# Four 64x64 products at a step's head for the last taps of two layers

## The chip, the cores and the metric

The kernel runs on one core of a Trainium2 chip. The core has five engines that run side by side, each through its own list of instructions in order: TensorE (PE in the profile, its weight loads PEld), VectorE (DVE), ScalarE (ACT), GpSimd (POOL) and SyncE (SP), which here issues most of the transfers. They wait for each other through semaphores. The metric is the device time of one execution in microseconds; the time of a version is the median of its runs.

## What is computed

Input x has 16 images of 64 channels of 128x128, in float32. Four layers follow, each a residual step on a group norm (`_gn`, 32 groups):

```python
x = x + _L0_conv_ref(_gn(x), conv_w)      # gram matrix of the channels, its product with x, a 64x64 mix
x = x + _L1_conv_ref(_gn(x))              # |Sobel x| + |Sobel y| of each channel
x = x + _L2_conv_ref(_gn(x), W, b)        # shift of channel groups by one column, 3x3 convolution
x = x + _L3_conv_ref(_gn(x), w_bin, ...)  # 3x3 convolution, 1x1, batch norm over all images, clip
```

Layer 3's batch norm needs all images, so the output can only be made in a closing pass over everything.

## The kernel before

An image is cut into eight pieces of rows (`NS` = 8), one per step. A long pipeline runs over the steps (loop at line 1059); in each step three stages work at different images or pieces: `Front` (layers 0 and 1) from step 15, `Layer2` from step 25, `Layer3` from step 35, each eight steps per image; the last of layer 3 is step 162. `Gram` prepares layer 0 for later images. A step has four quarters `q` = 0 to 3; in each quarter the stages run in the order Layer3, Layer2, Front, then Gram, and each engine keeps the order in which the program issues. After every quarter `tick` (264) advances the short chains that make the norms' coefficients.

- **Front.** From image 3 on (`self.four`, line 555) `mix_four` (579) mixes one piece in quarter 1: four products on 64x64 tiles of TensorE, written to the PSUM tiles `po` and `g`, which have one buffer each. `prepare` (598) lets ScalarE normalize them into `xh`: half 0 in quarter 2, half 1 in quarter 0 of the next step. The image's edge lines `pe` are handled once per image. `sobel` (657) is VectorE's work of layer 1 in all quarters, with the two absolute values on ScalarE.
- **Layers 2 and 3.** The 3x3 convolution over row pairs is rewritten with a product shared by both rows (`shared`, 750, into `one`) and two of its own (`own`, 753, into the two halves of `two`), on differences of rows (`diffs`, tiles `d2` and `d3`, made by `difference` on VectorE). Each product exists for two column halves of TensorE, and two halves of different sides run as a pair at a time; `issue` (730) pairs them and holds a rest back until a partner comes. In each `own`, one side has three taps. The other side reads only one row plane, that is half of the contraction; two of its taps are packed into one product (`pk`) with the help of a shifted copy (`twins`, tiles `qd`), and the last tap remains as a product of its own with half of its weights zero. `pk` and this last tap are the two entries of `some[o]` (line 757 on).
- **Twins.** Layer 3's are copied by ScalarE (952): two copies in quarter 3, two in quarter 0. Layer 2's come by two transfers on GpSimd's queue (810), after VectorE has made the difference: half 0 in quarter 0, half 1 at the end of quarter 3.
- **Order on TensorE in a step:** layer 3's shared and first own products (quarter 0), its second (1), the mixing (1), Gram products if any, layer 2's shared and one own (2), its other own (3).
- **Order on ScalarE:** quarter 0: two `qd<-d` copies, `xh` half 1, `junk<-u`; quarter 1: `c` of layer 3, `v` of layers 3 and 2; quarter 2: two absolute values, `c` of layer 2, `junk<-x`, `xh` half 0; quarter 3: two `qd<-d` copies, `junk<-y`. Copies `xw` for the Gram products come in between.
- **Order on VectorE:** quarter 0: two Sobel operations, the edge addition `two<-two,edges` and layer 2's result `x<-two,c`, `d2`; quarter 1: four Sobel operations; quarter 2: layer 3's result `y<-two,c`, `d3`, Sobel; quarter 3: `d3`, Sobel, `d2`.

The tiles `two` have two buffers, taken in turn by layers 3 and 2. Nearly all instructions go through the helper class `InOrder`, so the profile puts them at its line 73.

Of the kernel before, what the change touches and what calls it, by code (L numbers as in the profile page):

```python
# [16 lines left out]
P = 128  # L17
# [3 lines left out]
R = 8  # L21
# [23 lines left out]
def single(table, n):  # L45

    for o in range(2):
        planes = [i for m, i, half, _ in table if (m, half) == (n, o)]
        if len(planes) == 1:
# [3 lines left out]

NAMES = [("I", P), ("same", P), ("all", P), ("gavg", P), ("gmean", P), ("bnavg", P), ("Id", C), ("q", 1),
         ("keep0", 1), ("keep1", 1), ("left", 1), ("right", 1), ("I3", 3 * P), ("lower", 1), ("upper", 1)]
# [22 lines left out]
def constants():  # L78
    k = np.zeros((P, K_END), np.float32)
    p = np.arange(P)  # L80
    ch = p % C

    def put(name, a):
        k[:, AT[name][0]:AT[name][1]] = a

    same = ch[:, None] == ch[None, :]
    pair = ch[:, None] // 2 == ch[None, :] // 2
    put("I", np.eye(P))
    put("same", same)
    put("all", np.full((P, P), 0.5))  # L90
    put("gavg", 0.25 * pair)
    put("gmean", pair / (2.0 * HW))
    put("bnavg", (ch[:, None] == (p // 2)[None, :]) / (B * HW))
    put("Id", ch[:, None] == np.arange(C)[None, :])
    put("q", 0.25)
    put("keep0", (~((ch >= C // 4) & (ch < C // 2)))[:, None])
    put("keep1", (~(ch < C // 4))[:, None])

    left, right = ch < C // 4, (ch >= C // 4) & (ch < C // 2)
    put("left", left[:, None])  # L100
    put("right", right[:, None])
    put("I3", np.concatenate([np.eye(P) * m[:, None] for m in (left, ~left & ~right, right)], axis=1))
    put("lower", (p < C)[:, None])
    put("upper", (p >= C)[:, None])
    return k
# [3 lines left out]
def tile_kernel(ctx: ExitStack, tc: tile.TileContext, x, cw_h, w2_t, b2, wbin_t, w1_t, b1, gamma, beta, consts, out):  # L109
# [10 lines left out]
    def k(name):  # L120
        return kc[:, AT[name][0]:AT[name][1]]

# [96 lines left out]
    for name in ("d2", "d3"):  # L219
        diffs[name] = wpool.tile([P, 2, CP, W + 2], F32, name=name)  # L220
        pool.memset(diffs[name], 0.0)
        twins[name] = wpool.tile([P, 2, CP, W + 2], F32, name=f"q{name}")
        pool.memset(twins[name], 0.0)
# [10 lines left out]

    wm = wpool.tile([P, 3, P], F32, name="wm")
    packed = {}

    def other_weights():
        for n in range(2):
            o = 1 - single(TO_SLOTS, n)[0]  # L240
            pool.tensor_copy(wm[:, :, cols(o)], w2[:, n, :, cols(o)])

        for name, w, table in (("pk2", w2, TO_SLOTS), ("pk3", w3, TO_PAIRS)):
            dve.tensor_add(w[:, 2], w[:, 0], w[:, 1])
            packed[name] = wpool.tile([P, 2, C], F32, name=name)
            for n in range(2):
                o, i = single(table, n)
                for kx, half in ((1, i), (0, 1 - i)):
                    pool.tensor_copy(
                        packed[name][half * C:(half + 1) * C, n], w[i * C:(i + 1) * C, n, kx, o * C:(o + 1) * C]  # L250
                    )
# [17 lines left out]

    def rstd(mE, r, me, eps=None):  # L270

        dve.tensor_copy(me, mE)
        nv = sv("nv")
# [14 lines left out]
    def coefficients(st, put, back=None):  # L288
# [5 lines left out]
        pm = sm(2)  # L294
        small_product(pm, k("gmean"), s2)
        yield
        co = sv("co", 2) if back is None else sv("co2", 6)
        me = sv("me", 2)
        r, mean = co[:, 0:1], me[:, 0:1]
        yield from rstd(pm, r, me, GN_EPS)  # L300
        dve.scalar_tensor_tensor(co[:, 1:2], mean, -1.0, r, op0=ALU.mult, op1=ALU.mult)
# [11 lines left out]
    def gram_chain(b, pg):  # L313
# [21 lines left out]

        junk0 = stp.tile([P, C], F32, tag="junk0", name=f"junk0_{b}", bufs=1)
        dve.scalar_tensor_tensor(
# [56 lines left out]
        yield  # L394
        pp = stp.tile([P, 2, C], F32, tag="pp", name=f"pp_{b}", bufs=1)
        dve.tensor_mul(
# [152 lines left out]
    class Front:  # L549
# [29 lines left out]
        def mix_four(self, i):  # L579
# [3 lines left out]
            t = self.xs.pop(i)  # L583
            order = 1 - last[0], last[0]
            for g in range(2):
                for h in order:
                    pe.matmul(self.po[i, g][cols(h)], self.abd[cols(g), cols(g)], t[cols(g), h], start=True, stop=True)

# [17 lines left out]
        def at(self, i, q):  # L606
            b = self.b
            if q == 0:
# [6 lines left out]
                if i + 3 < NS and i + 3 not in self.xs:  # L615
                    self.load(i + 3)
                if -1 <= i < NS - 1:
                    self.prepare(i + 1, 1)
# [6 lines left out]
                if i == NS:  # L625
                    chains.append(coefficients(self.st, lambda co: coefs2.update({b: co}), b2_sb))
            if q == 1 and -2 <= i < NS - 2:
                if i == -2:
                    self.abd, self.co = lead.pop(b)
                if i == -2 and not self.four:  # L630
                    self.pe = ps_g.tile([P, CP, W], F32, tag="g", name=f"pe_{b}")[:, 0, :]
                    small_product(self.pe, self.abd, self.xe)
                if self.four:
                    self.mix_four(i + 2)
                else:
                    self.mix(i + 2, 0)
            if q == 3 and i == -2 and self.four:
                self.pe = ps_po.tile([P, CP, W], F32, tag="po", name=f"pe_{b}")[:, 0, :]
                small_product(self.pe, self.abd, self.xe)
            if (i, q) == ((-1, 0) if self.four else (-2, 2)):  # L640
                nc.gpsimd.memset(self.chunk(0)[lo, 0, :], 0.0)
# [3 lines left out]
            if q == 2:  # L645
                if i == NS - 2:
                    nc.gpsimd.memset(self.chunk(NS - 1)[hi, R + 1, :], 0.0)
                    act.copy(self.chunk(NS - 1)[lo, R + 1, 1:1 + W], self.pel[lo])
            if 0 <= i < NS:
                self.sobel(i, q)  # L650
            if q == 2 and -2 <= i < NS - 2:
                self.prepare(i + 2, 0)
            if q == 3 and -2 <= i < NS - 2 and not self.four:
                self.mix(i + 2, 1)
                self.xs.pop(i + 2)

# [72 lines left out]

    def issue(halves):  # L730


        for o in range(2):
            for n, (dst, wt, src) in enumerate(halves[o]):
                held[o].append((dst, wt, src, n == 0, n + 1 == len(halves[o])))
        while held[0] and held[1]:
            o = 1 - last[0]
            emit(o)
            emit(1 - o)
# [12 lines left out]

    def own(p, n, table, wt, name, m=CP, both=None):
        d, q, pk = diffs[name][:, n, 0:m], twins[name][:, n, 0:m], packed[f"pk{name[1]}"][:, n]
        o, _ = single(table, n)
        some = [None, None]
        some[1 - o] = taps(1 - o, p[:, 0:m], [wt[:, n] if both is None else both], [d], 1)
        some[o] = [
            (p[cols(o), 0:m], pk, q[:, :, 1:1 + W]),
            (p[cols(o), 0:m, 0:W - 1], wt[:, n, 2, cols(o)], d[:, :, 2:1 + W]),  # L760
        ]
        issue(some)


    tiles3 = {}

    class Layer2:
# [41 lines left out]

        def twin(self, n):  # L810

            d, q = diffs["d2"], twins["d2"]
            _, i = single(TO_SLOTS, n)
            pool.dma_start(flat(q[cols(i), n]), flat(d[cols(i), n]))
            pool.dma_start(
                flat(q[cols(1 - i), n])[:, 1:CP * (W + 2)], flat(d[cols(i), n])[:, 0:CP * (W + 2) - 1]
            )
# [15 lines left out]
        def at(self, i, q):  # L833
# [3 lines left out]
            if q == 0:  # L837
# [15 lines left out]
                if 0 <= i < NS:  # L853
                    difference("d2", 0, self.v[i], m)
                    self.twin(0)
            if q == 1:
# [28 lines left out]
            if q == 2:  # L885
                if 0 <= i < NS:
# [8 lines left out]
                    both = self.wi[:, 1]  # L895
                    own(two[:, 1], 1, TO_SLOTS, w2, "d2", m, both)
                    if closing:

                        p = two[:, 1, m:CP]
                        issue([taps(0, p, [both], [t[:, R:R + 1, :]]), taps(1, p, [both], [t[:, R - 1:R, :]])])  # L900

# [6 lines left out]
            if q == 3:  # L908
                if 0 <= i < NS:
                    t = self.v.pop(i)  # L910
                    two, one = self.p[i]
                    both = self.wi[:, 1]
                    own(two[:, 0], 0, TO_SLOTS, w2, "d2", m, both)
                    if closing:
                        p, srcs = two[:, 0, m:CP], [t[:, R - 2:R - 1, :], t[:, R - 1:R, :]]
                        issue([taps(0, p, [w2[:, 0], both], srcs), taps(1, p, [both, w2[:, 1]], srcs)])
            if q == "last of 0" and i == NS:
                self.square(i - 1)
            if q == "last of 3" and -1 <= i < NS - 1:
                difference("d2", 1, self.v[i + 1], CP if i + 2 < NS else CP - 1)  # L920
                self.twin(1)


    class Layer3:
# [34 lines left out]
        def at(self, i, q):  # L959
            b = self.b  # L960
            n = b * NS + i
            if q == 0 and 0 <= i < NS:
                self.twin(1)
                t = self.v[i]
                one = ps_one.tile([P, CP, W], F32, tag="one", name=f"one3_{b}_{i}")
                two = ps_two.tile([P, 2, CP, W], F32, tag="two", name=f"two3_{b}_{i}")
                self.p[i] = two, one
                shared(one, w3[:, 2], t)
                own(two[:, 0], 0, TO_PAIRS, w3, "d3")
            if q == 1:  # L970
                if 0 <= i < NS:
                    two, one = self.p[i]
                    own(two[:, 1], 1, TO_PAIRS, w3, "d3")
                    self.v.pop(i)
# [84 lines left out]
    for step in range(starts[2][1] - 2, steps):  # L1059
        now[0] = step  # L1060
        for q in range(4):
            for b in range(B):

# [127 lines left out]
```

## Time and profile before

| what | value |
|---|---|
| time, median of 3 runs | 2729.09 us (2726.27 to 2729.88) |
| span of the profiled execution | 2727.2 us |
| PE busy | 2162.2 us (79%) |
| DVE busy | 2170.0 us (80%) |
| ACT busy | 2079.2 us (76%) |
| POOL busy | 852.7 us (31%) |
| first and last `y<-two,c` | 321.6 and 2275.0 us |
| mean granted TensorE clock | 0.899 |

The first 320 us fill the pipeline; up to about 2280 us the steps run; then a closing pass loads, scales and stores all images and its transfers fill the DMA engines (420 GB/s). In the profile's lines a matrix product in float32 appears as two instructions (two passes); "64*64 64x512" means weights of 64 rows by 64 columns and 512 streamed columns, "128*64" a product over all rows into one column half. A line of the timeline has start, duration, engine, line, operation, output and inputs, and, in brackets, how long the engine sat idle before and what ended that.

### The profile page before, as it was taken

To read this page: it belongs to the slowest core of one execution; us is meant where nothing else is said; L and a number is where in the kernel's file an instruction comes from. 1 tells how busy PE (TensorE), PEld (TensorE's weight loads), DVE (VectorE), ACT (ScalarE), POOL (GpSimd) and SP (SyncE) were. 2 spreads that over 40 slices of the span, in tenths; PEclk is the share of its full clock that TensorE was granted. 3 is DMA by queue.
4 is the path that set the end of the run, shared out by engine and by line. 5 is a ranking of instruction groups with operands and counts; after the bars stand their busy time and mean duration, and the time that the engine had idled before them with its cause. 6 is when DMAs were issued, how large, how long until landed. Compare 5 with 4: busy or idle time off the path is not lost. (4 is left out here: it accounts for less than half of the span.)

```text
span 2727.2 us, 45742 instructions
## 1 busy us (share of the span) xinstructions
PE 2162.2 (79%) x14804; PEld 913.7 (34%) x14804; DVE 2170.0 (80%) x3495; ACT 2079.2 (76%) x3065; POOL 852.7 (31%) x1350
## 2 busy tenths in 40 slices
PE   6578899999999999999999999999999993000000
PEld 4234433434343434343434343333334641000000
DVE  4999999899999999999999999999995335333332
ACT  4766889898989898989898989899997667333332
POOL 2045424443434243333343334445453200000000
PEclk8689999999999999999999999999999996555555
DMA  8799878888888888888888887888877868999999
GB/s 199 205 239 239 226 197 239 225 235 225 235 228 237 227 226 229 226 227 234 225 224 237 214 204 203 207 211 216 224 200 186 226 188 314 420 420 420 420 420 385
DMA packets 693598, 685.93 MB, mean 252 GB/s; under 512 B 60096, under 2 KB 580448, under 8 KB 693360
## 3 DMA queue, kind: packets, MB, share of 16 engines
q1 hardware_dynamic: 668208, 613.83, 76.4%
q0 software_dynamic: 25152, 69.18, 10.0%
q8 instruction: 119, 1.95, 0.3%
q14 instruction: 119, 0.97, 0.1%
HBM read 346.23 MB, written 268.44 MB: 225 GB/s over the span
## 5 line engine op out<-in xcount | busy, mean ns | idle before, releaser
L73 PE MATMUL two<-d,w 128*64 128x508 f32 (+2 forms) x2560 | 848.9, 587 | 0.0
L73 PE MATMUL two<-d,wi 128*64 128x508 f32 (+3 forms) x1536 | 573.8, 577 | 0.0
L73 PE MATMUL two<-qd,pk 128*64 128x512 f32 (+1 forms) x1024 | 520.0, 589 | 24.5 <-DMA qd<-d 16.6
L73 POOL DMA_DIRECT2D qd<-d x512 | 271.1, 532 | 852.8 <-DVE d L73 323.9
L73 POOL TENSOR_SCALAR edges<-v,co 64x8 f32<-64x8 f32 x512 | 340.2, 664 | 349.0 <-ACT v L73 216.8
L73 DVE TENSOR_TENSOR d<-v 128x512 f32<-128x512 f32 (+1 forms) x512 | 346.6, 680 | 65.3 <-issue 37.5
L73 PEld LDWEIGHTS two<-d,w 128*64 128x64 f32 x2560 | 278.7, 136 | 320.0 <-issue 270.9
L73 PE MATMUL one<-v,w 128*64 128x508 f32 (+2 forms) x1600 | 364.3, 579 | 1.1 <-ACT v L73 1.1
L73 PE MATMUL one<-v,wi 128*64 128x508 f32 (+3 forms) x1536 | 353.3, 591 | 2.0 <-issue 1.4
L73 ACT COPY qd<-d 64x512 f32<-64x512 f32 x512 | 315.4, 616 | 19.9 <-DVE d L73 13.8
L73 DVE SCALAR_TENSOR_TENSOR e<-e 128x1032 f32<-128x1032 f32 (+1 forms) x256 | 313.0, 1223 | 0.0
L73 ACT ACTIVATE xh<-po,co 128x128 f32<-128x128 f32 (+1 forms) x480 | 275.9, 624 | 23.9 <-PE po L73 21.4
L73 PEld LDWEIGHTS two<-d,wi 128*64 128x64 f32 x1536 | 178.0, 135 | 197.4 <-issue 180.0
L73 DVE SCALAR_TENSOR_TENSOR y<-two,c 128x1024 f32<-128x1024 f32 x128 | 156.0, 1219 | 97.8 <-ACT v L73 45.6
L73 POOL TENSOR_SCALAR v<-v,kc 128x9 f32<-128x9 f32 x256 | 213.4, 847 | 12.0
L73 PE MATMUL po<-x,abd 64*64 64x512 f32 (+1 forms) x1024 | 177.1, 640 | 45.6 <-ACT xh L73 42.2
L73 ACT ACTIVATE v<-x,co 128x1024 f32<-128x1024 f32 (+3 forms) x256 | 203.8, 847 | 0.0
L73 ACT ACTIVATE u<-u 128x1024 f32<-128x1024 f32 x128 | 135.5, 1059 | 75.6 <-DVE u L73 74.6
L73 PEld LDWEIGHTS two<-qd,pk 128*64 128x64 f32 x1024 | 131.6, 135 | 176.9 <-issue 85.5
L73 PEld LDWEIGHTS one<-v,w 128*64 128x64 f32 x1600 | 130.9, 136 | 175.3 <-issue 146.5
L73 ACT ACTIVATE c<-one,co 128x512 f32<-128x512 f32 x128 | 86.7, 678 | 127.4 <-PE one L73 124.0
L73 DVE SCALAR_TENSOR_TENSOR u<-xh 128x1170 f32<-128x1170 f32 x128 | 175.4, 1370 | 4.2 <-ACT xh L73 4.1
(165 smaller groups left out, 3325.2 us busy)
## 6 DMA issues: line engine op xcount, KB each, us to landing
x<-in_x SPq DMA_DIRECT2D x256, 256.0 KB, 4.6
x_d<-u SPq DMA_DIRECT2D x512, 128.0 KB, 4.0
y_d<-y SPq DMA_DIRECT2D x512, 128.0 KB, 3.8
x_d<-x SPq DMA_DIRECT2D x496, 128.0 KB, 2.7
xr<-in_x SPq DMA_DIRECT2D x120, 512.0 KB, 5.9
qd<-d POOLq DMA_DIRECT2D x256, 130.0 KB, 3.3
qd<-d POOLq DMA_DIRECT2D x256, 129.8 KB, 3.8
v<-x_d SPq DMA_DIRECT2D x448, 72.1 KB, 3.0
```

What stands on the lines that cost most here:

```text
L73: return self.tc.keep_in_program_order(call(*args, **kwargs))
```

## The change

The last tap of the halved side leaves `own`. It becomes a 64x64 product, without the zero half, that adds to the same PSUM tile. Layer 2's two lie on the tiles (rows 0, columns 0) and (rows 1, columns 1) and read the shifted twin with weights `wl`; layer 3's two lie on the other diagonal and read `d3`. They are collected in `blocks` together with the four mixing products and issued at the head of the step, in a new phase "ahead" before quarter 0: first layer 2's, which end the sums of the step before, then layer 3's, which begin the sums of this step, then the mixing. So layer 3's `two` is taken at the head, layer 2's `two` ends one phase later, `mix_four` moves from quarter 1 to the head, and `prepare(.., 1)` from quarter 0 of the next step to quarter 3 (behind layer 3's part of that quarter); the edge lines of `pe` move from quarter 0 to quarter 3 as well. Images 0 to 2 keep their mixing. `issue` learns that a sum was begun before or will be ended later (`open_before`, `open_after`). Half 1 of layer 2's twin gets two places in turn, because its last tap is read a step later.

For room, two constants go (`gmean` becomes `gavg` with a scale in `rstd`, `Id` a part of `same`), `junk0` shares `t0`'s place and `pp` that of `dd`.

```diff
     def other_weights():
         for n in range(2):
-            o = 1 - single(TO_SLOTS, n)[0]
-            pool.tensor_copy(wm[:, :, cols(o)], w2[:, n, :, cols(o)])
+            o, i = single(TO_SLOTS, n)
+            pool.tensor_copy(wm[:, :, cols(1 - o)], w2[:, n, :, cols(1 - o)])
+            pool.tensor_copy(wl[cols(1 - i)], w2[cols(i), n, 2, cols(o)])
...
-        dve.tensor_copy(me, mE)
+        dve.tensor_scalar_mul(me, mE, scale)
...
             t = self.xs.pop(i)
-            order = 1 - last[0], last[0]
             for g in range(2):
-                for h in order:
-                    pe.matmul(self.po[i, g][cols(h)], self.abd[cols(g), cols(g)], t[cols(g), h], start=True, stop=True)
+                for h in range(2):
+                    blocks.append((self.po[i, g][cols(h)], self.abd[cols(g), cols(g)], t[cols(g), h], True, True))
...
-                if -1 <= i < NS - 1:
+                if -1 <= i < NS - 1 and not self.four:
                     self.prepare(i + 1, 1)
...
+            if q == "ahead" and self.four and -2 <= i < NS - 2:
+                if i == -2:
+                    self.abd, self.co = lead.pop(b)
+                self.mix_four(i + 2)
...
-            if q == 3 and -2 <= i < NS - 2 and not self.four:
-                self.mix(i + 2, 1)
-                self.xs.pop(i + 2)
+            if q == 3 and -2 <= i < NS - 2:
+                if self.four:
+                    self.prepare(i + 2, 1)
+                else:
+                    self.mix(i + 2, 1)
+                    self.xs.pop(i + 2)
...
+    blocks = []
+
+    def issue_blocks():
+
+        for dst, wt, src, start, stop in blocks:
+            pe.matmul(dst, wt, src, start=start, stop=stop)
+        if blocks:
+            last[0] = 1
+        blocks.clear()
...
-        some[o] = [
-            (p[cols(o), 0:m], pk, q[:, :, 1:1 + W]),
-            (p[cols(o), 0:m, 0:W - 1], wt[:, n, 2, cols(o)], d[:, :, 2:1 + W]),
-        ]
-        issue(some)
+        some[o] = [(p[cols(o), 0:m], pk, q[:, :, 1:1 + W])]
+        issue(some, [before and h == o for h in range(2)], [more or after and h == o for h in range(2)])
+
+    def place(n, m):
+
+        return n * (1 + m % 2)
+
+    def last_taps_of_2(two, m, size):
+
+        for n in range(2):
+            o, i = single(TO_SLOTS, n)
+            rows = cols(1 - i)
+            blocks.append((two[cols(o), n, 0:size, 0:W - 1], wl[rows], twins["d2"][rows, place(n, m), 0:size, 3:2 + W], False, True))
+
+    def last_taps_of_3(two):
+
+        for n in range(2):
+            o, i = single(TO_PAIRS, n)
+            rows = cols(i)
+            blocks.append((two[cols(o), n], w3[rows, n, 2, cols(o)], diffs["d3"][rows, n, :, 2:2 + W], True, False))
...
+            if q == "ahead" and 1 <= i:
+                last_taps_of_2(*self.tail)
...
+            if q == "ahead" and 0 <= i < NS:
+                one = ps_one.tile([P, CP, W], F32, tag="one", name=f"one3_{b}_{i}")
+                two = ps_two.tile([P, 2, CP, W], F32, tag="two", name=f"two3_{b}_{i}")
+                self.p[i] = two, one
+                last_taps_of_3(two)
...
     for step in range(starts[2][1] - 2, steps):
         now[0] = step
         for q in range(4):
+            if q == 0:
+                for stage, at in starts[1], starts[0], starts[2]:
+                    for b in range(B):
+                        run(stage, b, step - at - NS * b, "ahead")
+                issue_blocks()
```

More of the change, by code (lines that the diff above doesn't have):

```diff
@@ L50, in single @@
             return o, planes[0]
-NAMES = [("I", P), ("same", P), ("all", P), ("gavg", P), ("gmean", P), ("bnavg", P), ("Id", C), ("q", 1),
+NAMES = [("I", P), ("same", P), ("all", P), ("gavg", P), ("bnavg", P), ("q", 1),
          ("keep0", 1), ("keep1", 1), ("left", 1), ("right", 1), ("I3", 3 * P), ("lower", 1), ("upper", 1)]
@@ L91, in constants @@
     put("gavg", 0.25 * pair)
-    put("gmean", pair / (2.0 * HW))
     put("bnavg", (ch[:, None] == (p // 2)[None, :]) / (B * HW))
-    put("Id", ch[:, None] == np.arange(C)[None, :])
     put("q", 0.25)
@@ L120, in k @@
     def k(name):
-        return kc[:, AT[name][0]:AT[name][1]]
+        return kc[:, AT["same"][0]:AT["same"][0] + C] if name == "Id" else kc[:, AT[name][0]:AT[name][1]]
     def const(shape, name):
@@ L221, in tile_kernel @@
         pool.memset(diffs[name], 0.0)
-        twins[name] = wpool.tile([P, 2, CP, W + 2], F32, name=f"q{name}")
+        twins[name] = wpool.tile([P, 3 if name == "d2" else 2, CP, W + 2], F32, name=f"q{name}")
         pool.memset(twins[name], 0.0)
@@ L235, in tile_kernel @@
     wm = wpool.tile([P, 3, P], F32, name="wm")
+    wl = wpool.tile([P, C], F32, name="wl")
     packed = {}
@@ L268, in tick, with rstd @@
                 chains.remove(c)
-    def rstd(mE, r, me, eps=None):
-        dve.tensor_copy(me, mE)
+    def rstd(mE, r, me, eps=None, scale=1.0):
+        dve.tensor_scalar_mul(me, mE, scale)
         nv = sv("nv")
@@ L294, in coefficients @@
         pm = sm(2)
-        small_product(pm, k("gmean"), s2)
+        small_product(pm, k("gavg"), s2)
         yield
@@ L299, in coefficients @@
         r, mean = co[:, 0:1], me[:, 0:1]
-        yield from rstd(pm, r, me, GN_EPS)
+        yield from rstd(pm, r, me, GN_EPS, 2.0 / HW)
         dve.scalar_tensor_tensor(co[:, 1:2], mean, -1.0, r, op0=ALU.mult, op1=ALU.mult)
@@ L334, in gram_chain @@
         dve.tensor_copy(st[:, 0:1], mu)
-        junk0 = stp.tile([P, C], F32, tag="junk0", name=f"junk0_{b}", bufs=1)
+        junk0 = stp.tile([P, C], F32, tag="t0", name=f"junk0_{b}", bufs=1)
         dve.scalar_tensor_tensor(
@@ L394, in gram_chain @@
         yield
-        pp = stp.tile([P, 2, C], F32, tag="pp", name=f"pp_{b}", bufs=1)
+        pp = stp.tile([P, 2, C], F32, tag="dd", name=f"pp_{b}", bufs=1)
         dve.tensor_mul(
@@ L626, in at @@
                     chains.append(coefficients(self.st, lambda co: coefs2.update({b: co}), b2_sb))
-            if q == 1 and -2 <= i < NS - 2:
+            if q == "ahead" and self.four and -2 <= i < NS - 2:
                 if i == -2:
                     self.abd, self.co = lead.pop(b)
-                if i == -2 and not self.four:
+                self.mix_four(i + 2)
+            if q == 1 and -2 <= i < NS - 2 and not self.four:
+                if i == -2:
+                    self.abd, self.co = lead.pop(b)
                     self.pe = ps_g.tile([P, CP, W], F32, tag="g", name=f"pe_{b}")[:, 0, :]
                     small_product(self.pe, self.abd, self.xe)
[L633 to L636, printed above, removed]
+                self.mix(i + 2, 0)
             if q == 3 and i == -2 and self.four:
@@ L639, in at @@
                 small_product(self.pe, self.abd, self.xe)
-            if (i, q) == ((-1, 0) if self.four else (-2, 2)):
+            if (i, q) == (-2, 3 if self.four else 2):
                 nc.gpsimd.memset(self.chunk(0)[lo, 0, :], 0.0)
@@ L648, in at @@
                     act.copy(self.chunk(NS - 1)[lo, R + 1, 1:1 + W], self.pel[lo])
-            if 0 <= i < NS:
+            if 0 <= i < NS and q != "ahead":
                 self.sobel(i, q)
@@ L728, in emit, with issue @@
         last[0] = o
-    def issue(halves):
+    blocks = []
[5 more added lines that the diff above has]
+        blocks.clear()
+    def issue(halves, open_before=(False, False), open_after=(False, False)):
         for o in range(2):
             for n, (dst, wt, src) in enumerate(halves[o]):
-                held[o].append((dst, wt, src, n == 0, n + 1 == len(halves[o])))
+                first, end = n == 0, n + 1 == len(halves[o])
+                held[o].append((dst, wt, src, first and not open_before[o], end and not open_after[o]))
         while held[0] and held[1]:
@@ L751, in shared, with own @@
         products(p[:, 0:m], [wt], [by_parity(t)[1][:, 0:m]])
-    def own(p, n, table, wt, name, m=CP, both=None):
-        d, q, pk = diffs[name][:, n, 0:m], twins[name][:, n, 0:m], packed[f"pk{name[1]}"][:, n]
+    def own(p, n, table, wt, name, m=CP, both=None, at=None, after=False, more=False, before=False):
+        d, q, pk = diffs[name][:, n, 0:m], twins[name][:, n if at is None else at, 0:m], packed[f"pk{name[1]}"][:, n]
         o, _ = single(table, n)
@@ L808, in store, with twin @@
                 sp.dma_start(pairs(d, 0)[:, 0:1, :], t[lo, 1, CP - 1:CP])
-        def twin(self, n):
-            d, q = diffs["d2"], twins["d2"]
+        def twin(self, n, m):
+            d, q, at = diffs["d2"], twins["d2"], place(n, m)
             _, i = single(TO_SLOTS, n)
-            pool.dma_start(flat(q[cols(i), n]), flat(d[cols(i), n]))
+            pool.dma_start(flat(q[cols(i), at]), flat(d[cols(i), n]))
             pool.dma_start(
-                flat(q[cols(1 - i), n])[:, 1:CP * (W + 2)], flat(d[cols(i), n])[:, 0:CP * (W + 2) - 1]
+                flat(q[cols(1 - i), at])[:, 1:CP * (W + 2)], flat(d[cols(i), n])[:, 0:CP * (W + 2) - 1]
             )
@@ L854, in at @@
                     difference("d2", 0, self.v[i], m)
-                    self.twin(0)
+                    self.twin(0, i)
             if q == 1:
@@ L895, in at @@
                     both = self.wi[:, 1]
-                    own(two[:, 1], 1, TO_SLOTS, w2, "d2", m, both)
+                    own(two[:, 1], 1, TO_SLOTS, w2, "d2", m, both, place(1, i), True, closing)
                     if closing:
                         p = two[:, 1, m:CP]
-                        issue([taps(0, p, [both], [t[:, R:R + 1, :]]), taps(1, p, [both], [t[:, R - 1:R, :]])])
+                        issue([taps(0, p, [both], [t[:, R:R + 1, :]]), taps(1, p, [both], [t[:, R - 1:R, :]])], (True, True), (False, True))
                     self.c = ring.tile([P, CP * W], F32, tag="c2", name=f"c2_{b}_{i}", bufs=1)
@@ L912, in at @@
                     both = self.wi[:, 1]
-                    own(two[:, 0], 0, TO_SLOTS, w2, "d2", m, both)
+                    own(two[:, 0], 0, TO_SLOTS, w2, "d2", m, both, place(0, i), True, closing)
                     if closing:
                         p, srcs = two[:, 0, m:CP], [t[:, R - 2:R - 1, :], t[:, R - 1:R, :]]
-                        issue([taps(0, p, [w2[:, 0], both], srcs), taps(1, p, [both, w2[:, 1]], srcs)])
+                        issue([taps(0, p, [w2[:, 0], both], srcs), taps(1, p, [both, w2[:, 1]], srcs)], (True, True), (True, False))
+                    self.tail = two, i, m
+            if q == "ahead" and 1 <= i:
+                last_taps_of_2(*self.tail)
             if q == "last of 0" and i == NS:
@@ L920, in at @@
                 difference("d2", 1, self.v[i + 1], CP if i + 2 < NS else CP - 1)
-                self.twin(1)
+                self.twin(1, i + 1)
     class Layer3:
@@ L964, in at @@
                 t = self.v[i]
-                one = ps_one.tile([P, CP, W], F32, tag="one", name=f"one3_{b}_{i}")
-                two = ps_two.tile([P, 2, CP, W], F32, tag="two", name=f"two3_{b}_{i}")
-                self.p[i] = two, one
+                two, one = self.p[i]
                 shared(one, w3[:, 2], t)
-                own(two[:, 0], 0, TO_PAIRS, w3, "d3")
+                own(two[:, 0], 0, TO_PAIRS, w3, "d3", before=True)
             if q == 1:
@@ L972, in at @@
                     two, one = self.p[i]
-                    own(two[:, 1], 1, TO_PAIRS, w3, "d3")
+                    own(two[:, 1], 1, TO_PAIRS, w3, "d3", before=True)
                     self.v.pop(i)
```

## The prediction

> **What bounds the kernel now.** I read the page first, then the wait table, the busy time by stretches, and the timelines of TensorE (PE), VectorE (DVE) and ScalarE (ACT) over single steps. The page's chain of waits begins near 2226 us; from 2278 us it is transfers of the closing pass, which is bound by DMA and starts when layer 3 has ended, so it shifts one for one. What counts is the pipeline of steps before. Two stretches of it:
>
> ```profile
> 600.00:800.00 200.00, 198.87 (x1506) 81.12 (x1504) 189.08 (x328) 177.40 (x273) 71.24 (x123) 1.00 0.87 224
> 1600.00:1800.00 200.00, 196.06 (x1036) 71.16 (x1034) 196.87 (x309) 177.26 (x277) 88.96 (x131) 1.00 0.81 204
> ```
>
> Columns: length, then busy time of PE, weight loads, DVE, ACT, POOL, then granted clock. In the first stretch, with the Gram products of later images, PE is full (99%) and DVE has 5.5% left; in the second, without them, DVE is full (98%). No engine has much room, so what an edit does to the order of waits counts as much as the work it removes.
>
> The starts of `y` (one per step) give the pace: step 37 at 360.86 us, step 44 at 473.75, step 111 at 1576.47, step 140 at 2026.42. That is 103 steps in 1665.6 us: 16.46 us each between steps 44 and 111, 15.5 after. The 27 steps with Gram products are those of images 7 to 15, three each. Now one step of ScalarE and of TensorE:
>
> ```profile
> 2013.13 0.67 ACT L73 ACTIVATE c<-one,co 128x512 f32<-128x512 f32 x1
> 2013.70 1.04 ACT L73 ACTIVATE junk<-x 128x1024 bf16<-128x1024 f32 x1
> ...
> 2014.74 1.12 ACT L73 ACTIVATE xh<-po,co 128x512 f32<-128x512 f32 x2
> 2015.75 1.25 ACT L73 COPY qd<-d 64x512 f32<-64x512 f32 x2
> 2017.02 1.06 ACT L73 ACTIVATE junk<-y 128x1024 bf16<-128x1024 f32 x1
> ...
> 2018.20 1.24 ACT L73 COPY qd<-d 64x512 f32<-64x512 f32 x2
> 2019.47 1.13 ACT L73 ACTIVATE xh<-po,co 128x512 f32<-128x512 f32 x2
> ```
>
> ```profile
> 2016.07 2.73 PE L73 MATMUL one<-v,w 128*64 128x512 f32 x12
> ...
> 2023.00 1.09 PE L73 MATMUL po<-x,abd 64*64 64x512 f32 x8
> 2024.02 2.79 PE L73 MATMUL one<-v,wi 128*64 128x512 f32 x12
> ...
> 2030.92 0.60 PE L73 MATMUL one<-v,w 128*64 128x512 f32 x2
> ```
>
> See two things. TensorE's step starts at 2016.07 (layer 3), and the mixing comes at 2023.00. ScalarE empties the second mixing bank (the second `xh<-po`, 2019.47 to 2020.60) over four microseconds after the head and 2.4 us before the mixing needs it. That slack is what the change spends.
>
> **The change part by part.** *The four blocks.* A pair of half products (both column halves, two passes) occupies 0.85 us: eight pairs of layer 3 without a mixing behind them took 6.83 us (2030.92 to the next `one` at 2037.75). The last taps of the four owned halves filled two pairs, 1.70 us a step. The mixing takes from 2023.00 to 2024.02, 1.02 us for two passes of four 64x64 products, 0.51 a round. After: two such groups, 2.04 us. TensorE's own work falls by 1.70 + 1.02 - 2.04 = 0.68 us a step.
>
> The Trainium skill ("TensorE: Matmul & The Clock Gate", Part 3, "The mechanism") has packed products cost one product plus some 4 ns each, and also says that a weight load overlaps running products only in another row group. The second half speaks against the change, since four 64x64 tiles occupy all rows: a round took 0.51 us against 0.427 for a pass of a pair, so the row sides with it. By the first half alone a group would be 0.85 us, and my sum some 17 us lower.
>
> *The mixing moved to the head.* Its tiles `po` and `g` have one buffer each. `mix_four` of one step must wait until ACT has read them in the step before; the last reader is `prepare(.., 1)`, moved to the end of ACT's third quarter, behind `junk<-y`, where the copies `qd<-d` stood at 2018.20. Behind the waiting product on TensorE's queue stands all of layer 3, then layer 2's `one`; and ACT's `c<-one` of layer 2 waits for that, with `junk<-x`, `xh`, `qd`, `junk<-y` and again `prepare(.., 1)` queued behind it. That closes a ring of one step:
>
> - mixing released to layer 3's first product: 0.05 (after the ACT read ending 282.42 the waiting `po` product started 282.47) + 1.02
> - layer 3, seven pairs: 6.83 - 0.85 = 5.98
> - layer 2's `one` until `c` starts: 1015.31 to 1018.10 = 2.79
> - `c` to the point behind `junk<-y`: 2013.13 to 2018.20 = 5.07, and the `xh` pair 1.13
>
> Sum 16.04, say 16.05 us. Before, the ring ran from mixing to mixing without layer 3 in it: 1.02 + 2.79 + 5.07 + 1.24 (the `qd` copies ahead of `xh`) + 1.13 + 0.05 = 11.3 us, below the 14.36 us that the quickest steps take. Gram products lie between layer 3 and layer 2 and enter the ring:
>
> ```profile
> 1012.51 2.97 PE L73 MATMUL bank<-xw 128*64 128x65 f32 x88
> 1015.31 2.75 PE L73 MATMUL one<-v,wi 128*64 128x512 f32 x12
> ```
>
> 2.80 us there, 2.70 for the parts of 84: 2.75. Sum: 103 x 16.05 + 27 x 2.75 = 1727.4 us, against 1665.6: **+62**. TensorE's own step, with the second half of the mixing alone after its wait, is 16.05 minus about 1.0 of idling, so the 0.68 us saved is swallowed in the wait. DVE needs 14.36 us and what its chains add, so it stays inside 16.05.
>
> The ring's unknown is its length. From below 15.9: `junk<-x` (1.04) is absent in one step of eight, two `xh` lines (0.34) in one each. From above 16.4: the image's edge lines (two of 0.45), small chain products and copies `xw` of 1.19 ahead of `c`. These nearly cancel; I keep 16.05. The ends give +46 and +98.
>
> *The last taps in steps without mixing.* In the twelve steps 141 to 152 only layers 2 and 3 run, at 13.68 us; TensorE is full there, and 1.70 becomes 1.02: **-8**. In the last steps only layer 3 is left:
>
> ```profile
> 2235.86 1.23 DVE L73 SCALAR_TENSOR_TENSOR y<-two,c 128x1024 f32<-128x1024 f32 x1 [5.38 <-issue]
> 2235.95 2.78 PE L73 MATMUL one<-v,w 128*64 128x512 f32 x12 [0.19 <-ACT v L73]
> ...
> 2237.01 1.29 DVE L73 TENSOR_TENSOR d<-v 128x512 f32<-128x512 f32 x2
> 2237.79 1.26 ACT L73 COPY qd<-d 64x512 f32<-64x512 f32 x2 [1.88 <-DVE d L73]
> ```
>
> Today `one` runs beside `y` and both `d`, 7.82 us a step. The blocks at the head read both `d`, which DVE makes after `y`; `one` is queued behind. New step: `y` and `d` 2.44 (2235.86 to 2238.30), wait and blocks 1.07, `one` 2.57, four pairs 3.41, to the next `y` 0.25: 9.74 us, 1.9 more over eight steps: **+15**.
>
> *Costed at nothing.* Layer 2's final addition on DVE now waits for blocks at the head; they run before the mixing waits, about a microsecond ahead of that addition (`two<-two,edges`, 2.44 us after DVE's `u<-xh`); without that cover it would cost up to their 1.02 a step, +105 us, but DVE has 1.5 us a step to spare in the longer ring. The scaled copy in `rstd` (150 ns before) and the shared constants and tiles sit in chains with steps to spare, between 0 and 4 us over the run. The two `wl` copies on POOL happen once. The third `qd` slot keeps POOL's early transfer from waiting for the late last tap. The input loads of `x` keep their place on SP's queue and land 4.6 us after issue, a step ahead of the mixing.
>
> Total: 62 - 8 + 15 = +69 on the profiled 2727.2 us, 2796. That execution is 1.9 us under the median shown, so 2798.
>
> **The rivals.** *Faster:* ScalarE reaches `prepare(.., 1)` before TensorE has finished layer 2, and the ring never binds. Then 0.68 us comes off where TensorE is last (67 steps, 16.46 to 15.78, above DVE's 94.6% or 15.57: -45), and where DVE is last only its 2% (29 steps: -8), -2 in the first seven, -8 and +15 at the end: 2679 us. For it: DVE and TensorE busy shares leave that room. Against: it needs `junk<-y` to end 1.13 us before the blocks; at 2018.20 it ended two microseconds after the head. It decides once ACT's part from `c` falls below about 5.2 us, from 6.2.
>
> *No change:* the ring closes only through layer 3's `c`: copies and norms from `c` to `prepare` 11.5, plus 1.07 + 2.8, 15.4 us, with Gram steps at TensorE's own 17.8: 76 x 15.4 + 27 x 17.8 = 1651, -15 - 8 + 15, 2721. Against: layer 2's `c` already waited 1.69 us for its `one` at 1018.10.
>
> *Worse:* the idle microsecond per step lowers the granted clock from 1.00 to 0.96 (seen between 280 and 320 us, beside similar gaps), 0.4 us on the ring's 9.8 us of TensorE: +41, 2839. Against: at 2237 to 2252 the gaps of 0.2 to 0.5 us left it at 1.00.
>
> *The groups do not run four at once:* 1.02 us more a step, which the idle microsecond swallows, and 12 in steps 141 to 152: 2810.
>
> **How the numbers follow.** Ring as computed, grouped or not: 0.74, at 2798, its own range 2770 to 2830. Worse: 0.08. Faster: 0.14. No change: 0.04, being any mixture that lands within 0.2% (5.5 us, about what this kernel's runs can tell apart). So slower 0.82, same 0.04, faster 0.14. The range 2745 to 2842 holds the first two and the short ends of the ring, leaving out the faster case.
>
> **What would show it.** Right: `po` waiting for ACT `xh` in nearly every step, at about 1 us; steps of about 16 us without Gram products and 18.8 with; DVE's share down to some 90%; layer-3-only steps near 9.7 us. Wrong: `po` at the head without a wait, or steps at 14.4 to 15.

## The result, and the profile after

The changed kernel takes 2878.2 us (median of 4 runs, 2869.7 to 2879.5), the kernel before 2729.5: a ratio of 1.054, 95% interval [1.053, 1.056]. Slower was forecast, but by half as much: 2798 us, with 2842 as the upper end. The profiled execution has a span of 2875.3 us, 148.1 over before.

The same two stretches in the profile after (length, busy time of PE, weight loads, DVE, ACT, POOL, granted clock, DMA share, GB/s):

```profile
600.00:800.00 200.00, 189.16 (x1276) 69.95 (x1274) 179.72 (x293) 171.93 (x265) 66.29 (x119) 0.99 0.81 211
1600.00:1800.00 200.00, 190.32 (x1234) 69.29 (x1232) 185.66 (x308) 167.57 (x262) 67.12 (x121) 1.00 0.76 194
```

Two lines of the wait table, before and then after (total wait, times, longest):

```profile
ACT c L73 <- PE one L73: 137.8, 54, 4.9
...
PEld po L73 <- ACT xh L73: 51.1, 23, 6.3
```

```profile
ACT c L73 <- PE one L73: 299.0, 196, 4.3
...
PEld po L73 <- ACT xh L73: 214.4, 126, 6.9
```

No engine is full any more. TensorE went from 99 to 95% in the first stretch, VectorE from 98 to 93% in the second. In place of that, ScalarE waits more than before for TensorE (`c` for `one`) and TensorE for ScalarE (the weight loads of `po` for `xh`): a ring.

One step of it, in the timeline of ScalarE and of TensorE after:

```profile
1039.43 0.69 ACT L73 ACTIVATE c<-one,co 128x512 f32<-128x512 f32 x1 [0.65 <-PE one L73]
1040.02 1.05 ACT L73 ACTIVATE junk<-x 128x1024 bf16<-128x1024 f32 x1
...
1041.06 1.12 ACT L73 ACTIVATE xh<-po,co 128x512 f32<-128x512 f32 x2
1042.06 1.24 ACT L73 COPY qd<-d 64x512 f32<-64x512 f32 x2
1043.33 1.06 ACT L73 ACTIVATE junk<-y 128x1024 bf16<-128x1024 f32 x1
...
1044.38 1.11 ACT L73 ACTIVATE xh<-po,co 128x512 f32<-128x512 f32 x2
...
1055.49 0.69 ACT L73 ACTIVATE c<-one,co 128x512 f32<-128x512 f32 x1 [0.76 <-PE one L73]
```

```profile
1043.63 1.03 PE L73 MATMUL po<-x,abd 64*64 64x512 f32 x4
1045.55 1.08 PE L73 MATMUL po<-x,abd 64*64 64x512 f32 x4 [0.88 <-ACT xh L73]
1046.55 2.78 PE L73 MATMUL one<-v,w 128*64 128x512 f32 x12
...
1052.70 2.75 PE L73 MATMUL one<-v,wi 128*64 128x512 f32 x12
```

Follow it round: `c` at 1039.43, four operations, the second `xh` ends at 1045.49; the second half of the mixing, four instructions by itself, has waited 0.88 us and starts at 1045.55; layer 3 at 1046.55, layer 2 at 1052.70, and the next `c` at 1055.49, when its `one` ends. One round is 16.06 us.

Where the 148 us arose, by the starts of `y` in both traces:

| stretch | before | after | more | forecast |
|---|---|---|---|---|
| to step 37 | 360.9 | 365.0 | 4.1 | 0 |
| steps 38 to 140 | 1665.6 | 1778.7 | 113.2 | 62 |
| 141 to 152 | 163.1 | 160.3 | -2.8 | -8 |
| 153 to 162, layer 3 alone | 85.5 | 116.0 | 30.5 | 15 |
| after the last `y` | 452.2 | 455.3 | 3.1 | 0 |

### The profile page after: what moved, and what is told of

It reads as the page before. It is cut to its first block, busy times and chain, and to the rows that moved or that the text cites. A ratio compares the mean times of both kernels' runs of the same rounds, so it can differ in the third digit from the quotient of the medians.

```text
span 2875.3 us, 46182 instructions
## 1 busy us (share of the span) xinstructions
PE 2212.9 (77%) x14804; PEld 837.5 (29%) x14804; DVE 2180.5 (76%) x3495; ACT 2083.7 (72%) x3065; POOL 805.2 (28%) x1352
## 5 line engine op out<-in xcount | busy, mean ns | idle before, releaser
L73 PE MATMUL two<-d,w 128*64 128x508 f32 (+2 forms) x2048 | 619.1, 599 | 22.2 <-DVE d L73 20.2
L73 PE MATMUL two<-d,wi 128*64 128x508 f32 (+3 forms) x1536 | 471.2, 577 | 0.0
L73 POOL TENSOR_SCALAR edges<-v,co 64x8 f32<-64x8 f32 x512 | 278.0, 543 | 529.8 <-ACT v L73 222.8
L73 PE MATMUL one<-v,w 128*64 128x508 f32 (+2 forms) x1600 | 394.0, 629 | 0.0
L73 PE MATMUL po<-x,abd 64*64 64x512 f32 (+1 forms) x1024 | 287.2, 645 | 132.2 <-ACT xh L73 112.3
L73 PEld LDWEIGHTS two<-d,w 128*64 128x64 f32 (+1 forms) x2048 | 173.0, 135 | 264.1 <-issue 247.6
L73 POOL TENSOR_SCALAR v<-v,kc 128x9 f32<-128x9 f32 x256 | 227.7, 902 | 11.9
L73 PEld LDWEIGHTS two<-d,wi 128*64 128x64 f32 x1536 | 148.5, 136 | 197.5 <-issue 179.4
L73 ACT ACTIVATE c<-one,b_sb 128x512 f32<-128x512 f32 x128 | 87.8, 686 | 148.8 <-PE one L73 148.8
L73 PEld LDWEIGHTS one<-v,w 128*64 128x64 f32 x1600 | 110.3, 146 | 284.1 <-issue 266.2
```

The lines of the kernel that those rows point to most:

```text
L73: return self.tc.keep_in_program_order(call(*args, **kwargs))
```

## Experiments

**1. Is it the mixing's place, or the last taps?** Two kernels take the change apart. `mixing_back` is the changed kernel with the mixing and its reads where they stood before. Two places of its edit (the removed call stood in phase "ahead", the new one stands in quarter 1):

```diff
-                self.mix_four(i + 2)
...
+                if self.four:
+                    self.mix_four(i + 2)
...
-                if -1 <= i < NS - 1 and not self.four:
+                if -1 <= i < NS - 1:
                     self.prepare(i + 1, 1)
```

> The changed kernel with the mixing and the reads of its tiles put back where they stood before (mixing in quarter 1, second read in quarter 0); the four last taps stay at the head as 64x64 products. Ring theory (the mixing at the head closes a ring of about 16 us through layer 3, layer 2 and ScalarE): the ring is open again, steps without Gram products fall back to about 14.4 to 15.5 us, and the time is 2690 to 2730 us, with only the slower layer-3-only steps left. Rival (the last taps as 64x64 products at the head, or their mode on TensorE, cost the time): it stays above 2820 us.

`mixing_ahead_alone` is the kernel before with nothing but that move.

> The kernel before with only the mixing moved to the head and the second read of its tiles to quarter 3; last taps stay in the own products. Ring theory: the ring is one pair (0.85 us) longer than in the changed kernel, 16.9 us a step without Gram products, so 2860 to 2930 us, and the layer-3-only steps stay at 7.8 us. Rival (last taps): within 20 us of the kernel before.

Measured: 2747.1 us, ratio to before 1.0054 [1.0037, 1.0071], and 2917.8 us, ratio 1.069 [1.067, 1.071]. The move alone costs more than the whole change, and without it the change costs 18 us, a little above the 2690 to 2730 that were expected. The ring's length follows too. Two rounds of `mixing_ahead_alone`:

```profile
1487.07 1.08 PE L73 MATMUL po<-x,abd 64*64 64x512 f32 x4 [0.88 <-ACT xh L73]
1488.07 2.78 PE L73 MATMUL one<-v,w 128*64 128x512 f32 x12
...
1503.89 1.07 PE L73 MATMUL po<-x,abd 64*64 64x512 f32 x4 [0.89 <-ACT xh L73]
1504.90 2.78 PE L73 MATMUL one<-v,w 128*64 128x512 f32 x12
```

16.82 us from one to the next, against 16.9 expected. The last taps of layer 3 still stand in the ring here as one pair more, and the wait is the same 0.88 us. Layer-3-only steps stayed at 7.82 us, so the last stretch belongs to the last taps.

**2. Shortening the ring.** Two kernels take ScalarE's work out of it. `read_early` moves the second read of the mixing tiles up to quarter 2, directly behind the first; `square_behind_read` moves `junk<-y` behind it:

```diff
             if q == 2 and -2 <= i < NS - 2:
                 self.prepare(i + 2, 0)
-            if q == 3 and -2 <= i < NS - 2:
                 if self.four:
                     self.prepare(i + 2, 1)
...
```

```diff
-                if 0 <= i < NS:
+            if q == "last of 3" and 0 <= i < NS:
                     act.activation(
                         junk, self.y[i].rearrange("p s j w -> p (s j w)"), AF.Square,
...
```

> The changed kernel with ScalarE's second read of the mixing tiles moved from quarter 3 to quarter 2, directly behind the first. Ring theory: qd and junk<-y (2.44 us) leave the ring, which falls to about 13.6 us, below what TensorE and VectorE need, so 2680 to 2730 us. Rival (last taps): no change from 2878 beyond 20 us.

> The changed kernel with ScalarE's junk<-y moved behind the second read of the mixing tiles, so that 1.18 us leave the ring and nothing else changes. Ring theory: steps of 15.95 us fall by 0.9 to 1.2 us to what TensorE itself needs with the mixing in two halves (15.06), steps that were longer than the ring before the change keep their length; 2800 to 2840 us. Rival (mixing and reads cost by their order as such, not by the ring's length): 2865 us or more.

Measured: 2780.4 us, ratio 1.018 [1.017, 1.020], and 2781.2, ratio 1.019 [1.017, 1.020]. The first misses its 2680 to 2730 by 50 us, the second lies 19 under its 2800 to 2840. Some 100 us come back by the order of one ScalarE operation, with the last taps and the mixing untouched at the head. Steps that took 15.95 us after the change take 14.63 in both. That is 0.4 us below the 15.06 expected, for the second half of the mixing now follows the first at once; in `square_behind_read` all eight instructions stand in one line without a wait, and layer 3 starts 1.52 us after their first (2.92 in the round shown above, 1043.63 to 1046.55):

```profile
1813.33 1.60 PE L73 MATMUL po<-x,abd 64*64 64x512 f32 x8
1814.85 2.78 PE L73 MATMUL one<-v,w 128*64 128x512 f32 x12
```

`read_early` takes another 1.26 us out of the ring and gains nothing more; both stop some 33 us above `mixing_back`. By the starts of `y` most of it lies in the steps beside the Gram products (25 of 32 us between steps 37 and 140 in `read_early`): step 71 takes 18.5 us in both, and 16.40 in `mixing_back`. In the like place an image earlier, TensorE runs a whole step in 16.93 us in `read_early` (blocks at 789.68 and 806.61) without waiting, while VectorE's `d` waits 1.75 us (at 788.69). What holds it was not tried. Some of the rest is the clock, the subject of experiment 3: step 78 takes 17.13 us in `read_early` at a granted clock of 0.90, step 70 takes 15.51 at 1.00.

**3. The granted clock.** Some steps without Gram products took 17.8 us instead of 16. The timeline of the changed kernel shows how one of them differs from the round above:

```profile
1027.95 1.17 PE L73 MATMUL po<-x,abd 64*64 64x512 f32 x4 [1.14 <-ACT xh L73]
1029.05 4.34 PE L73 MATMUL one<-v,w 128*64 128x512 f32 x12
```

The same twelve products take 4.34 us, not 2.78, after a wait of 1.14, and the granted clock is 0.50 from 1028.8 to 1032.2 us (0.62 in the mean from 1028.9 to 1033.3). Two kernels put small unused products into an idle corner of PSUM, between the halves of the mixing:

```diff
         for n, (dst, wt, src, start, stop) in enumerate(blocks):
+            if n == 6 and len(blocks) == 8:
+                filler(16)
             pe.matmul(dst, wt, src, start=start, stop=stop)
```

`filler` does so in every step, and has 36 of them ahead of the last taps where layer 3 is alone; `filler_some` only at the heads of steps that had been long (its condition on the step is left out above).

> The changed kernel with 16 small products into an unused corner of a PSUM bank between the two halves of the mixing, where TensorE stands idle about a microsecond, and 36 of them ahead of the last taps in the steps of layer 3 alone, where it stands 2.1 to 2.6 us. Theory that idling lowers the granted clock and that this makes the steps of 17.9 us (instead of 16) and 12.9 (instead of 9.8): granted clock 1.00 in the steps, no steps of 17.9 without Gram products, 2800 to 2835 us. Rival (those steps are longer for another reason, or the ring alone makes all of it): 2875 us or more.

> The changed kernel with the 16 small products between the halves of the mixing only at the heads of the steps that were 17.8 us long without Gram products or a closing piece in them (step numbers 2 and 3 modulo 8, later also 0), none at the end. Clock theory: those steps come to 16.1 us with a granted clock of 1.00 in them, other steps stay, 2850 to 2868 us. Rival (they are long for another reason): 2875 us or more.

`filler` gave 2871.2 us, ratio 1.052 [1.050, 1.054], above the 2800 to 2835 expected: 7 us in all, although its granted clock was 1.00 between 400 and 2100 us. Its products cure and cost: steps 74 and 75 fall from 17.77 and 17.87 to 16.15 and 14.58, but beside Gram products, where TensorE has no idle time for them, step 70 rises from 18.84 to 20.45 at a clock of 1.00. `filler_some` separates the two: 2848.4 us, ratio 1.044 [1.043, 1.046], just under the 2850 to 2868 expected. One of its heads:

```profile
1001.82 1.08 PE L73 MATMUL po<-x,abd 64*64 64x512 f32 x4 [0.71 <-ACT xh L73]
1002.83 2.78 PE L73 MATMUL one<-v,w 128*64 128x512 f32 x12
```

The mixing still waits for `xh`, and the products behind it are at full speed. By step 140 this trace is 21.2 us ahead of the changed kernel's; at least that much of the 113 is the clock. It may be some 28: at heads without these products the clock now falls in four steps where it had held (46, 54, 70 and 110: 0.92 in place of 1.00 over the step), and they are 6.7 us longer in all than in the changed kernel.

**4. The last steps.** In the changed kernel they are 9.83 us long or, six of nine, 11.3 to 12.9. First one of 12.9 in its timeline, then the same step in `tail_behind_one`, which is `mixing_back` with layer 3's last taps behind the shared products where layer 3 is alone:

```profile
2361.48 1.22 DVE L73 SCALAR_TENSOR_TENSOR y<-two,c 128x1024 f32<-128x1024 f32 x1 [7.39 <-issue]
...
2362.63 1.29 DVE L73 TENSOR_TENSOR d<-v 128x512 f32<-128x512 f32 x2
```

```profile
2363.46 2.47 PE L73 MATMUL two<-d,w 64*64 64x512 f32 x4 [2.12 <-DVE d L73]
2365.86 4.94 PE L73 MATMUL one<-v,w 128*64 128x512 f32 x12
```

```profile
2220.73 2.78 PE L73 MATMUL one<-v,w 128*64 128x512 f32 x12
2223.44 1.65 PE L73 MATMUL two<-d,w 64*64 64x512 f32 x5
```

> mixing_back, and in the steps where layer 3 is alone its last taps are issued behind the shared products instead of ahead of them. Theory of the last steps (the products at the head wait for both d of VectorE, with the shared products queued behind, and the idle time lowers the clock on top): these steps fall from 9.8 to 12.9 us back to 7.4 to 7.9, and the time by about 30 us to 2710 to 2722 us, under the kernel before. Rival (the 64x64 products themselves make those steps long): no change from 2747 beyond 6 us.

Measured: 2716.9 us, ratio to the kernel before 0.9959 [0.9947, 0.9972], against 2747.1 of `mixing_back`. The steps are 7.25 to 8.16 us long. So 30 us of the last stretch, the clock's part included, come from putting the products that need VectorE's `d` ahead of those that don't. Of the step of 12.9 us above, 3.1 are the clock: the last taps take 2.47 us and the shared products 4.94, where 1.58 and 2.78 are usual. In `filler`, with the order unchanged, those steps are 9.80 to 9.83 but for the first (13.08, with a granted clock of 0.66 from 2322 to 2327 us), and the stretch of steps 153 to 162 is 106.2 us instead of 116.0. With 9.83 for each of the nine it would be 103.0 (an estimate); so of the 30 us the order makes some 17 and the clock some 13.

`tail_behind_one` also says what the four 64x64 products are worth on their own: 12 us, 0.4% faster than before.

## Why the prediction was half right

**The ring.** Place, members, order and length were right: 16.05 us were worked out, 16.06 measured in the round shown, 16.9 and 16.82 with one pair more, 18.75 to 18.85 and 18.70 to 18.84 with Gram products. So was the claim that TensorE's saving would vanish in it.

**The sum made from the ring was the step that failed**: "Sum: 103 x 16.05 + 27 x 2.75 = 1727.4 us". It gives every step the ring's length, nothing more to steps that take longer and nothing to the clock. The prediction had listed reasons for other lengths and let them go: "These nearly cancel; I keep 16.05." The 1665.6 us of before were a sum over unequal steps. One image, by the intervals between the starts of `y`, steps 67 to 74:

| | 67 | 68 | 69 | 70 | 71 | 72 | 73 | 74 | sum |
|---|---|---|---|---|---|---|---|---|---|
| before | 14.36 | 14.64 | 16.35 | 15.20 | 17.03 | 20.40 | 17.64 | 16.16 | 131.8 |
| after | 16.25 | 15.95 | 16.41 | 18.84 | 18.70 | 20.24 | 17.96 | 17.77 | 142.1 |
| `mixing_back` | 14.36 | 14.63 | 16.35 | 15.20 | 16.40 | 19.81 | 17.64 | 16.16 | 130.6 |

Steps 68, 70 and 71 were lengthened to the ring's 16 and 18.8 us. Steps 69 and 74 were at it already (74's 17.77 is the clock). Steps 72 and 73 had been longer than the 18.8 and 16.05 of the sum and stayed so, at 20.24 and 17.96 us. Step 67 was short and stayed short: its 16.25 is 14.60 in `filler_some`. Taking, step by step, the larger of the ring and of what the step took before gives 1766.7 us for steps 38 to 140, 39 above the sum; the 13 steps like 67 take some 20 off again. So of the 51 us by which this stretch exceeded its forecast, the clock makes 21 to 28 (experiment 3) and steps longer than the sum's some 20, an estimate from these intervals.

The starts of layer 3's `one` at TensorE's head divide it in another way. From 1135.64 to 1274.44 us, where the clock is 1.00, eight rounds of the changed kernel take 138.8 us, and the sum has 136.65 for them (five of 16.05, three of 18.8). Seven of the eight heads wait for ScalarE, 0.47 to 1.78 us. In the longest round without Gram products, 17.56 us, ScalarE itself waits for VectorE: 0.82 us for `u` (at 1143.99) and 0.83 for `nv` (at 1148.62). No run changed these waits or what keeps steps 72 and 73 long; that the sum was short there is measured, its cause is only read from the traces.

The other 28 of the 79 us between forecast and result are 15 in the last steps, mostly the clock, 5 in steps 141 to 152, and 7 before step 38 and after the last `y`, which no run takes apart.

**The clock was a rival of its own, at 0.08**, "0.4 us on the ring's 9.8 us of TensorE: +41", as a uniform 0.96. That 0.96 of before, between 280 and 320 us, was already a mean: 0.50 from 307.7 to 311.1 us and 1.00 on both sides. The loss came together with the ring, not in its place, and in that form: most steps ran at 1.00, and some lost 1.6 to 3.3 us at once (steps 74 and 75 against `filler_some`). The argument against it, that gaps of 0.2 to 0.5 us had left the clock alone, used gaps shorter than the ring's own microsecond. The Trainium skill ("TensorE: Matmul & The Clock Gate", "HAM oscillation") warns of idle gaps over some 3.4 us; here gaps of 1.0 to 2.1 us stood before slow products, so the measurement decides.

**The last steps.** 9.74 us were worked out and 9.83 measured where the clock held. The missing term is again the clock: TensorE, idle for 2.1 us in the steps shown, lost it in six of nine.

**The four products.** Two groups were priced at 2.04 us; issued together they took 1.88 (789.68 to 791.56 in `read_early`), between that and twice the 0.85 us that the prediction took from the packing rule of the Trainium skill ("TensorE: Matmul & The Clock Gate", Part 3, "The mechanism"). In steps 141 to 152, where layer 2's two and layer 3's two stand without a mixing, one group took the 1.02 us worked out (2230.89 to 2231.91). What the prediction had not seen is how little that is worth: with the ring open, in `mixing_back`, steps 38 to 140 take 1653.2 us against 1665.6, 0.12 us a step, where 0.68 had been worked out for TensorE. The shortest steps stay at 14.3 us as before; that VectorE, 98% busy before, allows no less was not tried. The rival "faster" promised -55 us there and was wrong even where its condition holds. In steps 147 to 152, where TensorE is full, the step fell from 13.68 to 13.15, by 0.53; the first ones, 141 to 145, grew by 1.0 in all, so -2.8 and not -8.

**Costed at nothing and free:** layer 2's final addition, the shared constants and places, the `wl` copies. `mixing_back` contains all of them and its ordinary steps agree with those of before to 0.02 us.

## What to carry to other kernels

Work that is moved in an in-order queue takes its wait along, and all that is queued behind it waits too; look for the ring that this closes over one step, add up its members from the trace, and compare it with each kind of step: some are longer by themselves, and in some it does not bind. A small re-ordering of the engine that releases the wait can be worth more than the change itself: one ScalarE operation moved gave back 97 us. And time during which TensorE stands idle is not only lost but can slow what follows.

## What was not expected of the hardware

An idle gap of about one microsecond in 16 us of otherwise full work was enough to bring the granted clock down to 0.50 for 3.4 us (from 1028.8 us, after 1.14 us of idling; a gap of 1.78 us was followed by 0.50 from 441.8 to 448.5), but only in some of the steps with such a gap: after 0.88 us (at 1045.55) layer 3's shared products took 2.78 us, after 0.97 us (at 1938.79) 4.48, after 1.14 us (at 1027.95) 4.34, after 1.31 us (at 1905.65) again 2.78. The length of the one gap doesn't decide it alone; what does was not tried. Keeping TensorE occupied with useless products for part of the gap, with 0.71 us of it left, held the clock at 1.00 at that head.
